# Moving the stores of the fp8 adjacency chunks back in SyncE's order in a four-layer graph network on Trainium2

## Chip, cores and metric

The kernel runs on one core of one Trainium2 chip. The metric is the device time of one launch in microseconds (us). Before the change the median of three runs is 6208.64 us (6201.9 to 6210.01).

## The reference, cut to what matters

There are 16 graphs of 1024 nodes with 128 features and a 0/1 adjacency matrix each. Four layers follow one another, each with a residual and a layer norm:

```
x = layernorm(x + softmax(masked relu-attention(x, adj)) @ v)                    # layer 0
x = layernorm(x + max over neighbours j of relu(p_i + q_j + b), adj as mask)     # layer 1
x = layernorm(x + MLP((1 + eps) * x + adj^T x))                                  # layer 2
adj_d = dilate(adj)      # row by row, earlier removals change the later rows
x = layernorm(x + (3 x (SAGE on adj_d, relu, batch norm), concatenated) @ Wl + bl)  # layer 3
```

`dilate` walks through the rows of a graph one after another: it counts a row's edges, and if there are more than ten it removes those whose rank is a multiple of half the count, symmetrically in the column. It depends on the adjacency alone, so it can run beside layers 0 to 2.

## The kernel before

**Slots.** Layers 0 to 2 and the dilation run together in one long stage. Its clock is layer 1. For every graph the 1024 neighbours are cut into 86 groups of 12 (`NP`, `PS`), and one group is one *slot*; 16 x 86 = 1376 slots are written out one after the other by `slot(s, last)` (L861). In a slot ScalarE (ACT) turns a matmul of the adjacency (`count`, L805, from the tile `AT`) into one-hot rows `hot`; TensorE (PE) looks up the maxima of neighbour subsets with them (`look_up`, L837, into the PSUM tile `pg`, two buffers); and VectorE (DVE) merges them into `best` (L908), twice per slot.

**Adjacency chunks.** `AT` holds 120 neighbours (ten slots' worth) by 1024 nodes in fp8. A graph has nine chunks (the ninth has 64 rows), so there are 144 in all, in four buffers. `load_columns(at)` (L753) is called every tenth slot with the number of the chunk that is needed about twenty slots later. It issues the load of that chunk from GpSimd (POOL), which also casts it from the f32 input to fp8, and on SyncE (SP) a store of the *previous* chunk to the DRAM copy `adj8` (L758), which the last layer reads long after (L995). A buffer of `AT` is free for chunk n+4 when the matmuls of chunk n are done and its store has landed.

**The dilation** (`dilation`, L500) goes through 32 row blocks of 32 rows (43 slots each). POOL decides the rows of a block one by one (L669 to L679), after DVE has made `low` and `rest` (L653, L655). Then SP stores `hit` (L686) and loads it back spread over the partitions as `hit_p` (L689), and DVE transposes it (`hit_T`, L703). While POOL works at block k, DVE finds the removed edges of block k-1 (`remove`, L573): the tile `gone` (L613, two buffers) goes to DRAM through SP (`removed`, L615), and its transpose `last_T` (L620) also (`removed_T`, L622). Later blocks load `gone_T` back (L517). `Vp` and `V` (L555, L556) also pass through SP.

**Other work of SP**: the loads of X, the rows of a graph (`load_x`, L745; three buffers, so a load follows the store of an older graph's X, L466). PE transposes X at L290.

**What sets the order.** PE, ACT, DVE and POOL run in this stage in the order in which the code is written (`tc.manual_schedule`); a planner inside the kernel (`ask`, `advance`) only decides where each small step is written. SP is not in that list: the framework's scheduler chooses the order of SP's instructions from their dependencies and an own estimate of time. SP then works through that order one after the other, and each DMA is issued when the semaphores that it waits for have come. The helper `behind(ins, start)` (L237) adds a dependency that counts in the scheduler's ordering alone, without a semaphore: the instructions emitted since `start` come behind `ins`.

Of the kernel before, what the change touches and what calls it, by code (L numbers as in the profile page):

```python
# [39 lines left out]
B, N, D, H2 = 16, 1024, 128, 256  # L40
P = 128
T = N // P
GS = 6
PS = 2 * GS
PC = 10
CH = PC * PS
# [28 lines left out]
def tile_graph_layers(ctx: ExitStack, tc, a, out):  # L75
    nc = tc.nc
# [95 lines left out]
    for b in range(B):  # L172
        q, g = divmod(b, G)
        nc.gpsimd.dma_start(out=half_rows[g * R:(g + 1) * R, :, q],
                            in_=a["nodemask"][b].rearrange("(k r) -> r k", r=R))
# [21 lines left out]
    adj8 = [dram.tile([N, N], F8, name=f"adj8_{b}") for b in range(B)]  # L197
# [39 lines left out]
    def behind(ins, start):  # L237
        for i in nc.cur_bb.bb.instructions[start:]:
            tc.add_manual_dep(i, ins.name, mybir.DependencyInfo(
                mybir.DependencyClass.NoSync, mybir.DependencyReason.SCHED_ONLY), reason="pace")  # L240

    def layers_012():
# [133 lines left out]
        def attend(b):  # L376
            for t in range(T):
                yield ask("PE", 0.01, after=("e", b, t))
                if t == 0:
                    y = w4.tile([P, T, D], F32, name="y0", tag="xT")  # L380
                e, total = exps.pop((b, t))
                eT = w4.tile([P, T, P], F32, name="eT")
                for h in range(2):
                    yield ask("PE", 0.44, take=True, same=(h == 0))
                    p = shared("pe")
                    for c in range(4):
                        nc.tensor.transpose(p[:, c * P:(c + 1) * P],  # L387
                                            e[:, (4 * h + c) * P:(4 * h + c + 1) * P], ident)
                    yield ask("A", 0.59, give=True, same=True)
                    nc.scalar.copy(eT[:, 4 * h:4 * h + 4, :].rearrange("p c i -> p (c i)"), p)  # L390
                happened["back", b, t] = now
                for h in range(4):
                    yield ask("PE", 0.45, take=(h == 0), same=(h > 0))
                    if h == 0:
                        pav = shared("pav")[:, :D]
                    for c in range(2 * h, 2 * h + 2):
                        nc.tensor.matmul(pav, eT[:, c, :], values[b][:, c, :], start=(c == 0), stop=(c == T - 1))  # L397
                yield ask("V", 0.4, give=True)
                share = small.tile([P, 1], F32, name="share")
                nc.vector.reciprocal(share, total)  # L400
                nc.vector.scalar_tensor_tensor(y[:, t, :], pav, share, X[b][:, t, :], op0=ALU.mult, op1=ALU.add)
            yield from norm(X[b], y)
            happened["X1", b] = now
# [66 lines left out]
        def tables_of(b):  # L470

            if b:
                yield ask("V", 0, urgent=True, after=("tables", b - 1))
            for g0 in range(0, NP, TG):
                n_g = 2 * min(TG, NP - g0)
                yield ask("V", 0.01, same=True, urgent=True, after=("q", b))
                made.append((b, g0))
                yield ask("V", 0.1, same=True, urgent=True, after=("used", *made[-3]) if len(made) > 2 else None)
                qg = qs[b].rearrange("o (g s) -> o g s", s=GS)
                subs[b, g0] = w2.tile([P, TG, P], F32, name="sub", bufs=2)  # L480
                sub = subs[b, g0].rearrange("o t (a s) -> o (t a) s", a=2)
                nc.vector.memset(sub[:, :n_g, 0:1], LOWEST)
                for k in range(GS):
                    n = 1 << k
                    yield ask("V", 0.06 + n * n_g / 960, same=(n < 8), urgent=True)
                    nc.vector.tensor_max(sub[:, :n_g, n:2 * n], sub[:, :n_g, 0:n],  # L486
                                         qg[:, 2 * g0:2 * g0 + n_g, k:k + 1].to_broadcast([P, n_g, n]))
                happened["sub", b, g0] = now
            happened["tables", b] = now
# [255 lines left out]
        def load_x(b):  # L745
            X[b] = apool.tile([P, T, D], F32, name="X", bufs=3)
            nc.sync.dma_start(out=X[b], in_=x[b].rearrange("(t p) d -> p t d", p=P))
# [4 lines left out]

        def load_columns(at):  # L753
            b, c = divmod(at, T + 1)
            if at:
                before, k = divmod(at - 1, T + 1)
                rows = min(CH, N - k * CH)
                nc.sync.dma_start(out=adj8[before][k * CH:k * CH + rows], in_=AT[at - 1][:rows])  # L758
            if b < B:
                rows = min(CH, N - c * CH)  # L760
                t = AT[at] = apool.tile([CH, N], F8, name="AT", bufs=4)
                if rows < CH:
                    nc.gpsimd.memset(t, 0.0)
                nc.gpsimd.dma_start(out=t[:rows], in_=adjT[b, c * CH:c * CH + rows])

        An, AT, subs, qs, ps, values, exps, bests, hots, tables = ({} for _ in range(10))
# [8 lines left out]
        def start(stream, first=False):  # L775
            pending[stream] = [next(stream, None), -9]
            streams.insert(0 if first else len(streams), stream)
# [59 lines left out]
        def look_up(s, h, pg):  # L837

            at = s % 2
            for k, part in enumerate(tables[s - at]):  # L840
                for a in range(2):
                    rows = slice(64 * a, 64 * a + 64)
                    nc.tensor.matmul(pg[:, a], part[rows, at * P:(at + 1) * P], hots[s][rows, halves[h]],  # L843
                                     start=(k == 0), stop=(k == 1))
# [5 lines left out]
        def total(b, h):  # L850
            s = halves[h]
            nc.vector.tensor_add(ps[b][:, s], bests[b][:, 0, s], ps[b][:, s])

        def dilate_on():
            nonlocal due, wants_bank
            if due <= now and not (wants_bank and taken >= 2 and given.get(taken - 2, 1e9) > now):
                after, cost, wants_bank = next(dilate, (B * NP, 0, False))
                due += after
                room["V"] -= cost

        def slot(s, last):  # L861

            nonlocal now
            now = s
            b, g = divmod(s, NP)
            if s >= 0 and g == 0:
                bests[b] = bests[b - 1] if b else w4.tile([P, 2, N], F32, name="best")
                if b + 1 < B:
                    start(tables_of(b + 1), True)
                    load_x(b + 1)  # L870
                    start(attend(b + 1))
                    start(scores(b + 1))
            if s >= 0 and g % PC == 0 and b * (T + 1) + g // PC + 2 <= B * (T + 1):
                load_columns(b * (T + 1) + g // PC + 2)
            for h in range(2):
                now = s + 0.5 * h
                for e in ROOM:
                    room[e] = min(room[e] + ROOM[e] / 2, ROOM[e] / (2 if e in ("PE", "V") else 1))
                if s >= 0:
                    pg = psum.tile([P, 2, 512], F32, tag="wide", name="pg", bufs=2)  # L880
                    look_up(s, h, pg)
                early = s >= 0 and due < now
                if early:
                    dilate_on()
                advance(("PE",))
                advance(("A", "V", "Pool"))
                if s >= 0 and not early:
                    dilate_on()
                if h == 0 and s % 2 and s + 1 < last:
                    low_part(s + 1)  # L890
                if s + 2 < last:
                    count(s + 2, h)
                    if h and s % 2 == 0:
                        table(s + 2)
                if s >= 0:
                    own = bests[b][:, :, halves[h]]
                    if g == 0:
                        if b:
                            if h:
                                merge(b - 1, h)  # L900
                            total(b - 1, h)
                        nc.vector.tensor_copy(own, pg)
                        if b and h:
                            start(rest(b - 1))
                    else:
                        if g == NP - 1 and h:
                            merge(b, 0)
                        nc.vector.tensor_max(own, own, pg)  # L908
            if s >= 0:
                hots.pop(s)  # L910
# [460 lines left out]
```

## Time and profile before

| | |
|---|---|
| median of three runs | 6208.64 us |
| profiled execution | 6199.75 us |
| its span | 6198.0 us, 93287 instructions |
| PE | busy 5582.7 us (90%) |
| DVE | busy 4870.0 us (79%) |
| ACT | busy 3988.2 us (64%) |
| POOL | busy 3613.1 us (58%) |
| merges L908 on DVE | 2720 x 1214 ns |
| AT loads L764 on POOL | 144, median 3.9 us from issue to landing |
| stores of AT on SP (L758) | 144, median 333 ns to issue |

The span is that of one execution as the hardware profiler took it. Busy times are per engine and overlap. SP's instructions are DMA issues and aren't counted as busy, but they have their own list of waits: how long SP stood before an issue, and which event released it. A line such as "DVE x L613 <- DMA y<-z: 80.6, 9, 18.0" says that DVE stood still before the instruction of L613 that writes x, 80.6 us in nine times, 18.0 at the longest, until a DMA that reads z and writes y had landed. The slot stage runs from about 140 to 5085 us; the last layer's passes follow.

### The profile page before, as it was taken

The numbers are of one execution on the slowest core, as the hardware profiler recorded it, in microseconds if no ns is written. First come the engines' busy times: TensorE is split into PE (matmuls) and PEld (weight loads), VectorE is DVE, ScalarE is ACT, GpSimd is POOL, SyncE is SP. The second block draws the span as 40 slices with busy tenths as digits, with TensorE's granted clock in tenths as the row PEclk, the third lists the DMA queues.
The fourth block names the chain that finished last, engine by engine and source line by source line (L and its number), as shares of the span: only waits on it lengthen the run. The fifth ranks groups of instructions, "written<-read, shape, count | busy, mean of one in ns | idle before, by whom it ended". The sixth has DMA issues, their size and how long they took to land.

```text
span 6198.0 us, 93287 instructions
## 1 busy us (share of the span) xinstructions
PE 5582.7 (90%) x30144; PEld 3046.0 (49%) x30250; DVE 4870.0 (79%) x7484; ACT 3988.2 (64%) x7362; POOL 3613.1 (58%) x11879
## 2 busy tenths in 40 slices
PE   5989899989898989999989798989999878999998
PEld 4545454545454545454545454545444435555654
DVE  3888788888888888889888788888889875555455
ACT  3767676767676767677767576767666554344855
POOL 2676666667666767677777757667677651110114
PEclk8999999989999999999999899999999989999999
DMA  5021213121212212122121211212121014554645
GB/s 42 11 33 25 40 22 42 22 40 24 40 24 31 32 32 32 32 32 38 26 43 22 39 24 31 31 31 33 31 33 28 19 41 124 159 144 133 214 163 191
DMA packets 496976, 334.28 MB, mean 54 GB/s; under 512 B 303338, under 2 KB 448228, under 8 KB 492388
## 3 DMA queue, kind: packets, MB, share of 16 engines
q1 hardware_dynamic: 405504, 260.29, 14.5%
q0 software_dynamic: 89008, 67.42, 12.6%
q8 instruction: 237, 3.88, 0.3%
q14 instruction: 255, 2.09, 0.1%
q10 hardware_dynamic: 1972, 0.59, 0.1%
HBM read 362.38 MB, written 133.96 MB: 80 GB/s over the span
## 4 chain that ended last, share of the span: by engine, by line
PE 31%; DVE 10%; ACT 4%; POOL 3%; issue 2%; DMA 1%; SPq 0%; DVEq 0%; POOLq 0%; ACTq 0%
PE pg L843 7%; PE pagg L1071 5%; DVE best L908 5%; PE pm L812 3%; PE po L1101 2%; PE po L1095 1%; PE pa L439 1%; PE pav L397 1%; PE pp L300 1%; ACT hot L813 1%; PE pdeg L1026 1%; DVE near L1014 1%; PE psc L349 1%; PE prank L599 1%; PE pe L387 1%
## 5 line engine op out<-in xcount | busy, mean ns | idle before, releaser
L908 DVE TENSOR_TENSOR best<-best,pg 128x1024 f32<-128x1024 f32 x2720 | 3259.3, 1214 | 512.6 <-PE pg L843 501.7
L813 ACT ACTIVATE hot<-pm,one_less 128x512 fp32r<-128x512 f32 x2752 | 1887.4, 689 | 780.5 <-PE pm L812 773.2
L843 PE MATMUL pg<-hot,high 64*128 64x512 f32 x5504 | 1407.3, 508 | 258.9 <-DVE best L908 220.8
L843 PE MATMUL pg<-hot,low 64*128 64x512 f32 x5504 | 1115.5, 402 | 0.0
L812 PE MATMUL pm<-AT,lit 120*128 120x512 fp8e4 x2752 | 1085.9, 395 | 4.5 <-ACT low L834 3.5
L843 PEld LDWEIGHTS pg<-hot,high 64*128 64x128 f32 x5504 | 523.5, 187 | 1014.6 <-DVE best L908 492.8
L669 POOL TENSOR_SCALAR sc<-low_counts,half_mask,rest 16x1 f32<-16x1 f32 x992 | 354.4, 357 | 393.9 <-DVE rest L655 283.2
L843 PEld LDWEIGHTS pg<-hot,low 64*128 64x128 f32 x5504 | 537.9, 192 | 0.0
L812 PEld LDWEIGHTS <-lit 120*128 120x128 fp8e4 x2752 | 270.3, 98 | 389.8 <-issue 313.5
L674 POOL TENSOR_SCALAR sc<-sc 16x1 f32<-16x1 f32 x992 | 393.1, 396 | 105.1
L834 ACT CAST low<-pt 128x256 fp32r<-128x256 f32 x688 | 256.0, 372 | 263.3 <-PE pt L832 261.9
L671 POOL TENSOR_SCALAR sc<-sc 16x1 f32<-16x1 f32 x992 | 324.5, 327 | 107.6
L1116 POOL TENSOR_TENSOR length<-length,mhalf 128x8 f32<-128x8 f32 x48 | 78.9, 1644 | 489.2 <-DVE length L1115 489.2
L676 POOL TENSOR_SCALAR hit<-V,sc 16x31 bf16<-16x31 bf16 (+30 forms) x992 | 362.4, 365 | 0.0
L677 POOL TENSOR_SCALAR last_rank<-V,sc 16x31 f32<-16x31 bf16 (+30 forms) x992 | 342.9, 346 | 0.0
L832 PE MATMUL pt<-high,less 128*128 128x256 f32 x688 | 279.2, 406 | 67.6 <-ACT high L827 61.5
L824 PE MATMUL pt<-ident,sub 128*128 128x128 f32 x1376 | 277.5, 283 | 51.8 <-ACT hot L813 50.0
L486 DVE TENSOR_TENSOR sub<-sub,q 128x24 f32<-128x24 f32 (+11 forms) x768 | 304.0, 397 | 24.8 <-ACT q L304 10.4
L397 PE MATMUL pav<-v,eT 128*128 128x128 f32 x2048 | 301.5, 292 | 2.0 <-ACT eT L390 2.0
L397 PEld LDWEIGHTS pav<-v,eT 128*128 128x128 f32 x2048 | 255.4, 196 | 73.3 <-issue 55.7
L670 POOL TENSOR_SCALAR sc<-sc 16x1 f32<-16x1 f32 x992 | 237.0, 239 | 86.5
L349 PE MATMUL psc<-kT,qT 128*128 128x256 f32 x1024 | 276.3, 388 | 9.9 <-issue 9.9
(270 smaller groups left out, 9662.9 us busy)
## 6 DMA issues: line engine op xcount, KB each, us to landing
removed<-gone SPq DMA_DIRECT2D x128, 256.0 KB
An<-in_adj_dram POOLq DMA_DIRECT2D x16, 1024.0 KB, 16.0
E<-in_adj_dram POOLq DMA_DIRECT2D x128, 128.0 KB, 6.6
gone_all<-removed POOLq DMA_DIRECT2D x64, 256.0 KB, 10.2
near<-adj SPq DMA_DIRECT2D x16, 1024.0 KB
kept<-near SPq DMA_DIRECT2D x16, 1024.0 KB
share<-share SPq DMA_DIRECT2D x32, 512.0 KB
hidden<-r SPq DMA_DIRECT2D x32, 512.0 KB
```

What stands on the lines that cost most here:

```text
L349: nc.tensor.matmul(psc[:, 256 * i:256 * (i + 1)], qT[:, t * P:(t + 1) * P], kT[:, s.start + 256 * i:s.start + 256 * (i + 1)], start=False, ...
L397: nc.tensor.matmul(pav, eT[:, c, :], values[b][:, c, :], start=(c == 0), stop=(c == T - 1))
L669: gp.tensor_scalar(half, mine, half_mask[:, m], rest[:, n:n + 1], op0=ALU.mult, op1=ALU.add)
L671: gp.tensor_scalar(sf, half, 5.5, sf, op0=ALU.is_gt, op1=ALU.mult)
L674: gp.tensor_scalar(to, at, sf, none, op0=ALU.subtract, op1=ALU.subtract)
L676: gp.tensor_scalar(hit[:, n, n + 1:], V[:, n, n + 1:], at, None, op0=ALU.is_equal)
L677: gp.tensor_scalar(last[:, n + 1:], V[:, n, n + 1:], to, None, op0=ALU.is_le)
L812: nc.tensor.matmul(pm, lit[:, r, :], AT[b * (T + 1) + c][:, halves[h]], start=True, stop=True)
L813: nc.scalar.activation(hots[s][:, halves[h]], pm, AF.Relu, bias=one_less)
L843: nc.tensor.matmul(pg[:, a], part[rows, at * P:(at + 1) * P], hots[s][rows, halves[h]], start=(k == 0), stop=(k == 1))
L908: nc.vector.tensor_max(own, own, pg)
L1071: nc.tensor.matmul(pa[:, s], piece[:, t, :], m[c][:, s], start=(i == 0), stop=(i == 15))
```

## The change

`load_columns(at)` now stores chunk at-2 in place of chunk at-1: a store is emitted in the call 20 slots after the one with its chunk's load, instead of 10. In addition the store is tied by `behind` to the last instruction emitted ahead of it, of whichever engine, so the scheduler can't place it earlier in SP's order than that instruction. As the stores lag one more call, the condition in `slot` that ended the calls at the last chunk is dropped, which leaves one further call at the end that only stores.

```
         def load_columns(at):
             b, c = divmod(at, T + 1)
-            if at:
-                before, k = divmod(at - 1, T + 1)
+            if at > 1:
+                before, k = divmod(at - 2, T + 1)
                 rows = min(CH, N - k * CH)
-                nc.sync.dma_start(out=adj8[before][k * CH:k * CH + rows], in_=AT[at - 1][:rows])
+                begin = len(nc.cur_bb.bb.instructions)
+                nc.sync.dma_start(out=adj8[before][k * CH:k * CH + rows], in_=AT[at - 2][:rows])
+                behind(nc.cur_bb.bb.instructions[begin - 1], begin)
             if b < B:
...
-            if s >= 0 and g % PC == 0 and b * (T + 1) + g // PC + 2 <= B * (T + 1):
+            if s >= 0 and g % PC == 0:
                 load_columns(b * (T + 1) + g // PC + 2)
```

From L758 on the line numbers of the changed kernel are larger by one or two: the store is L759, the load L766, the merge L910.

## The prediction

> **What bounds the kernel now.** The change touches only DMAs that SyncE (SP in the profile) issues, in the stage from about 140 to 5085 us in which the slots run. In that stage PE is busy 4487.33 of 4945 us, DVE 4252.78 and POOL 3390.61 (the busy times of that stretch). So PE and DVE take turns as the bound: 1376 slots in 4945 us are 3.59 us a slot, and each slot holds PE look-ups and two DVE merges (L908), which wait for each other through two PSUM buffers. In such a pair a pause of one engine stops the other within one or two half-slots. I therefore read the waits first, and only those whose releaser is a DMA, since SP orders DMAs and nothing else. The list of waits of DVE, then of PE and of POOL, in that stage (us in total, times, longest):
>
> ```profile
> DVE best L908 <- PE pg L843: 501.7, 848, 20.3
> DVE gone L613 <- DMA removed<-gone: 80.6, 9, 18.0
> DVE hit_T L703 <- DMA hit_p<-hit: 23.6, 2, 14.4
> ...
> PE ptr L290 <- DMA X<-in_x_dram: 28.7, 4, 20.3
> ...
> POOL counts L546 <- DVE U L544: 119.2, 13, 22.0
> ```
>
> DVE stands still 80.6 us in nine places because the tile `gone` that it wants to overwrite (two buffers) has not been stored; PE stands still 28.7 us because X has not come. Both transfers are issued by SP. SP's own waits, over the whole run:
>
> ```profile
> SPq L758 <- DMA AT<-in_adjT_dram: 2846.5, 138, 54.8
> SPq L686 <- POOL hit L678: 463.6, 24, 29.7
> SPq L615 <- DVE gone L613: 372.7, 47, 19.4
> ```
>
> SP spends 2846.5 us at the stores of AT (L758), each waiting for a load that has not even been issued. What is queued behind pays. The timelines of SP and then of DVE round one stall (start us, us, what; in brackets the idle time before it and its releaser):
>
> ```profile
> 1871.07 0.33 SPq L758 DMA_DIRECT2D adj<-AT  x1
> 1871.46 0.38 SPq L615 DMA_DIRECT2D removed<-gone  x1
> 1871.93 0.39 SPq L622 DMA_DIRECT2D removed_T<-last_T  x1
> 1908.75 0.45 SPq L758 DMA_DIRECT2D adj<-AT  x1
> 1909.30 0.54 SPq L615 DMA_DIRECT2D removed<-gone  x1
> ...
> 1895.84 1.21 DVE L908 TENSOR_TENSOR best<-best,pg 128x1024 f32<-128x1024 f32 x1
> 1911.94 0.55 DVE L613 TENSOR_SCALAR gone<-rank,least,match 128x1024 bf16<-128x1024 f16 x1 [14.89 <-DMA removed<-gone]
> ```
>
> SP issues nothing from 1872.3 to 1908.75. The `gone` finished at 1868.4 is stored only at 1909.30, and DVE waits 14.89 us for it; PE's look-ups have a gap of 14.9 us there too. Likewise for X:
>
> ```profile
> 3524.22 0.34 SPq L466 DMA_DIRECT2D x<-X  x1
> 3548.01 0.32 SPq L758 DMA_DIRECT2D adj<-AT  x1
> 3548.43 0.40 SPq L747 DMA_DIRECT2D X<-in_x_dram  x1
> ...
> 3561.55 1.11 PE L290 MATMUL ptr<-ident,X 128*128 128x128 f32 x4 [20.32 <-DMA X<-in_x_dram]
> ```
>
> [...] during those 36 us no later SP transfer is issued although its data is ready. [...] here a look-up pair that takes 0.50 us takes 0.80 us directly after the 16.4 us gap at 650 us.
>
> **The change part by part.**
> (1) *Stores move back in SP's order.* In the program as built PE, DVE, ACT and POOL hold the same instructions in the same order as before. SP's 1082 other transfers keep their order too; only the 144 stores move, by 0 to 22 other transfers, 9 at the median. No instruction is added or removed, so the issue cost of 144 x about 0.33 us stays on SP.
> To price the move I went through SP's new order with the readiness times of the trace of before: the end of `gone` (L613), of `last_T` (L620), Vp (L552), the last `hit` of a row block (L678), and the POOL issue of each AT load plus its 3.9 us to landing (the median of the profile); an issue takes 0.45 us. The same walk over the old order meets the measured issues within 1.5 us for 95% of most kinds. Over the new order:
> - SP waits for an AT load at two of the 144 stores only (the first, and one at 391 us that nothing ready stands behind), against 138 before.
> - The `removed` stores are issued on average 9.0 us earlier, by up to 41 us. Before, 67 of 128 were over 3 us late; one stays so, in the last row block, where it stands behind `hit`. The nine DVE waits need at most 18.0 us. Each goes: **-80.6 us**.
> - The X loads of 3548.4 and 3869.6 us go out 21.5 and 20.0 us earlier. PE's two long waits for X in this stage are 20.3 us (at 3561.6) and 8.0 us (at 3874.4). X then lands at 3526.9 + 13.1 = 3540.0 by the landing time of before (3548.4 to 3561.5), and PE wants it at 3541.2: both go: **-28.3 us**.
> (2) *Does a removed stall shorten the run by as much?* Row blocks of the dilation take 43 slots each, and the nine `gone` stalls lie in nine of the 32 blocks. From `rest` (L655) to the next `rest`, those nine (blocks 3, 5, 7, 9, 11, 13, 19, 25, 27) take 165.7, 154.7, 160.3, 155.6, 159.7, 161.1, 147.3, 157.0 and 157.0 us; less their own stalls (18.0, 4.8, 9.1, 7.4, 14.9, 11.8, 4.7, 4.2, 5.8) they average 148.6. The five odd blocks without one from 15 on (15, 17, 21, 23, 29) average 149.0. So nothing is caught up after a stall, and I take one for one. [...]
> (3) *The wait that stays.* `hit_T`'s 23.6 us (9.3 at 408.8, 14.4 at 5045.6) comes from POOL, which ends its rows at 402.8 and 5040.0; SP issues `hit` at once both times. **0**.
> (4) *The longer hold of AT's buffers.* There are four. The load of chunk n+4, issued by POOL, needs the store of chunk n. In the walk that store is issued at least 9.9 us (chunk 7), in all other cases at least 27.6 us before POOL comes to the load (before: 100.6). A store of 120 KB that lands in the 3.9 us of its load is out of the way. **0**; if this cover is gone, POOL stands still in its row loop.
> (5) *SP traffic between `hit` and `hit_p`*, which DVE soon needs: a few AT stores now stand there, 0.45 us each, against slacks at `hit_T` of over 2 us in the blocks concerned: **0 to +5 us**. From below, [...] the few small waits for late stores: **-10 to 0**. They roughly cancel; I take 0.
>
> Sum: -80.6 - 28.3 = **-108.9 us**. The profiled execution of before took 6199.75 us (span 6198.0), so its like after is 6090.8. The median of the three runs is 6208.64, 8.9 above that execution; from it the change gives 6208.64 - 108.9 = 6099.7, so **6100 us**.
>
> **The rivals.**
> *A. POOL takes back much of it.* After a row block's 31 POOL rows come `hit`, `hit_p` and DVE's `hit_T`. In the stall blocks `hit_T` starts only 3.5 to 10.6 us after the last `hit_p` is issued, and a landing takes about 2.8. If POOL kept its times, DVE would wait there for what the stall exceeds that slack by: 16.1, 2.0, 2.2, 5.5, 14.2, 10.8, 0.3, 0.7 and 0 us, together 51.8. The gain is then 57 us: 6152 us. For it: POOL's row loop takes about 118 us of a block and is near the bound. Against it: POOL itself waits for DVE in just these blocks (the L546 line above; 22.0 us in block 3, 16.7 in block 11). Less its waits, POOL needs 115.1 to 119.9 us there, plus about 5.7 for both transfers (2.9 to the last issue, 2.8 to land), while `hit_T` would come 125 to 137 us after `rest`. Hence small.
> *B. Slower: POOL is held at AT loads.* A store now stands nearer the load that reuses its buffer, and where it is queued behind `hit` (SP waits there for POOL up to 29.7 us) a load may find its buffer taken. POOL issues in order, so its rows, `hit_T` and then DVE are late. It decides from the point where stores run 10 us (one chunk) or 28 us (the rest) later than the walk says. At 5 us in each of 32 blocks it costs 160 us: 6099.7 + 160 = 6260 us. Against it: those margins, and that all SP work in the walk gets earlier.
> *C. The stalls have another cause* [...], and one wait replaces another: no change, about 6207 us. Against it: in the nine stalls SP's preceding issue is an AT store, within 3 us of the stall's end.
>
> **How the numbers follow.** The main case gets 0.80 (its own range 6080 to 6125), A 0.14 (6125 to 6160), C 0.02, B 0.04. A measurement of this kernel tells about 0.2%, 12 us, from no change. Faster: 0.80 + 0.14 = 0.94; same 0.02; slower 0.04. The range runs from 6072 (the -10 of part 5, and as much again for small waits that go too) to 6150, just short of A's worked point.
>
> **What would show it.** Right: in the profile after, "DVE gone <- DMA removed" and the 20 us wait of PE for X are gone, SP's waits at AT stores fall from 2846 us to under 150, and the slot stage ends near 4976 instead of 5085. A shows as more than 40 us of "DVE hit_T <- DMA hit_p"; B as POOL waiting for "DMA adj<-AT" at L766. It is wrong if these stalls go and the stage is not about 100 us shorter.

## The result and the profile after

The changed kernel takes 6095.76 us (median of 4 runs, 6090.76 to 6098.93) against 6207.42 us before (4 runs): a ratio of 0.9821, 95% interval 0.9804 to 0.9838, or 111.7 us less. The profiled execution took 6090.76 us, its span 6089.0 us, 109.0 us less than before. Of these, 107.2 us lie in the slot stage: its last merge (L908, now L910) ends at 4982.0 us in place of 5089.3.

The waits of DVE from 140 to 5085 us, the window of before, which now takes in some 100 us of the last layer (in total, times, longest):

```profile
DVE best L910 <- PE pg L845: 470.4, 839, 8.8
DVE hit_T L703 <- DMA hit_p<-hit: 26.2, 2, 15.7
```

The line "DVE gone L613 <- DMA removed<-gone", 80.6 us before, has vanished. PE's list for the stage has no wait for X any more (28.7 us before). On DVE that wait of PE had shown as a wait for look-ups: its first line is 31.3 us shorter (501.7 to 470.4). So DVE's own list closes the account: 80.6 + 31.3 less the 2.6 us by which `hit_T` grew are 109.3 us. POOL's list:

```profile
POOL num L707 <- DVE counts L530: 289.6, 31, 21.6
POOL sc L669 <- DVE rest L655: 285.0, 30, 15.5
...
POOL counts L546 <- DVE U L544: 27.4, 11, 6.8
```

Its wait at L546, 119.2 us before, has shrunk to 27.4, so most of it was an echo of the stalls. SP's own list over the whole run:

```profile
SPq L615 <- DVE gone L613: 1874.2, 119, 53.9
SPq L686 <- POOL hit L678: 724.4, 24, 76.0
...
SPq L759 <- DMA AT<-in_adjT_dram: 41.5, 2, 34.1
```

SP waits nearly as long as before (5522 us against 5664, all lines of its list added up), but for something else: it stands at the store of `gone` until DVE has made it. That delays nobody: `hit_T` is the only wait for an SP transfer that DVE and PE still have in the stage. The 2846.5 us at the stores of AT have become 41.5 us, in the two places that the walk named. The timeline of SP in the row block of the prediction's example:

```profile
1813.79 0.34 SPq L615 DMA_DIRECT2D removed<-gone  x1
1815.67 0.38 SPq L622 DMA_DIRECT2D removed_T<-last_T  x1
1816.15 1.14 SPq L759 DMA_DIRECT2D adj<-AT  x1
1823.89 0.33 SPq L615 DMA_DIRECT2D removed<-gone  x1
```

Each `removed` goes out at once (DVE starts these two `gone` at 1813.2 and 1823.3 us, each takes 0.54 us), and SP issues the store of AT behind them without a wait for its load. Of the 128 `removed` stores 67 were over 3 us late before; now one is, in the last row block, as the walk said. The X load that was 21.5 us late now follows the store of the older X within 3 us and stands ahead of the AT store:

```profile
3451.25 0.34 SPq L466 DMA_DIRECT2D x<-X  x1
3453.98 0.40 SPq L747 DMA_DIRECT2D X<-in_x_dram  x1
3454.47 0.54 SPq L759 DMA_DIRECT2D adj<-AT  x1
```

### The profile page after: what moved, and what is told of

The parts are those of the page before. It is cut to its first block, busy times and chain, and to the rows that moved or that the text cites. A ratio compares the mean times of both kernels' runs of the same rounds, so it can differ in the third digit from the quotient of the medians.

```text
span 6089.0 us, 93282 instructions
## 1 busy us (share of the span) xinstructions
PE 5556.8 (91%) x30144; PEld 3035.5 (50%) x30250; DVE 4873.7 (80%) x7484; ACT 3992.1 (66%) x7362; POOL 3642.6 (60%) x11879
## 4 chain that ended last, share of the span: by engine, by line
PE 33%; DVE 11%; ACT 4%; issue 2%; POOL 1%; DMA 1%; SPq 0%; DVEq 0%; ACTq 0%; POOLq 0%
PE pg L845 8%; DVE best L910 5%; PE pagg L1073 5%; PE pm L814 3%; PE po L1103 2%; PE pa L439 1%; PE po L1097 1%; PE pav L397 1%; PE pp L300 1%; ACT hot L815 1%; DVE sub L486 1%; PE prank L599 1%; PE pdeg L1028 1%; DVE near L1016 1%; PE pe L387 1%
## 5 line engine op out<-in xcount | busy, mean ns | idle before, releaser
L910 DVE TENSOR_TENSOR best<-best,pg 128x1024 f32<-128x1024 f32 x2720 | 3260.8, 1215 | 481.2 <-PE pg L845 470.4
```

## The experiments

The theory: SP works through its order one after the other (36 us without an issue in the prediction's example), and an AT store ahead of its load holds up the `removed` stores and X loads behind it; DVE and PE then stand still, one for one. The rivals: POOL's chain takes the gain back (A), POOL is held at AT loads (B), another wait takes the place (C).

### The lag alone

Against the changed kernel one line goes; the lag of two calls stays:

```
                 nc.sync.dma_start(out=adj8[before][k * CH:k * CH + rows], in_=AT[at - 2][:rows])
-                behind(nc.cur_bb.bb.instructions[begin - 1], begin)
```

> The store is emitted a call later (chunk at-2), but not tied. Built so, SP holds its transfers in the same order as before the change: the scheduler puts the stores back ahead. If what counts is SP's order (my theory), nothing changes: about 6207 us, SP waits some 2850 us at the stores, DVE some 80 us for removed<-gone. If the later emission itself counts (buffers, POOL's loads), the time goes to about 6097 us.

Measured: 6201.39 us beside 6201.5 us of before on that chip, ratio 0.9997 (0.9988 to 1.0007). Its waits, DVE's in the stage and SP's in the run:

```profile
DVE gone L613 <- DMA removed<-gone: 84.8, 10, 18.1
...
SPq L759 <- DMA AT<-in_adjT_dram: 2859.5, 138, 55.2
```

Writing the store ten slots later in the code does nothing: SP is outside the manual schedule, and the scheduler puts the store back where it stood. In the trace SP's 1226 transfers come in exactly the order of before.

### The tie alone

Against the kernel before:

```
+                begin = len(nc.cur_bb.bb.instructions)
                 nc.sync.dma_start(out=adj8[before][k * CH:k * CH + rows], in_=AT[at - 1][:rows])
+                behind(nc.cur_bb.bb.instructions[begin - 1], begin)
```

> The store keeps its lag of one call (chunk at-1), but is tied behind the place where it is emitted. Going through SP's order as built with the readiness times of the changed kernel, SP waits about 110 us in all at the stores (24 of 144) and no ready transfer stands behind for long. My theory: all of the gain, 6090 to 6100 us. If the lag of 20 slots is needed, some of the stalls of DVE for gone return: 6120 us or more.

Measured: 6106.6 us, ratio 0.9838 (0.9817 to 0.9858), beside 6201.5 us of before on that chip: 94.9 us less; the interval is 88 to 113 us. No wait of DVE for `gone` or of PE for X is left, and at the stores SP waits:

```profile
SPq L759 <- DMA AT<-in_adjT_dram: 87.5, 24, 11.3
```

So the tie carries the change. The changed kernel's ratio, 0.9821, is 0.17% lower, but the two intervals overlap widely; whether the second lag adds a little stays open. This run also answers a doubt. In the profiled execution of the changed kernel PE is busy 23.7 us less in the slot stage than before (4465.1 us against 4488.8), and the mean granted clock of that stage is 0.98 in place of 0.96, so the clock could have had a part in the gain. With the tie alone PE is busy 4490.3 us there, no less than before (granted clock 0.965 over the whole execution, against 0.962 in the trace of before), and the stage still ends 92.6 us earlier (at 4996.7 us).

### The tie in the first half of the graphs

As the tie alone, but only the chunks of graphs 0 to 7 are tied:

```
+                if before < 8:
+                    behind(nc.cur_bb.bb.instructions[begin - 1], begin)
```

> The tie (lag of one call) only for the chunks of graphs 0 to 7; the others as before. In the walk through SP's order the stalls of DVE for gone up to 2220 us go (18.0 + 4.8 + 9.1 + 7.4 + 14.9 + 11.8 = 66.0 us), and those at 3111, 4052 and 4360 us and PE's two waits for X stay. If each stall counts one for one: 6207 - 66 = 6141 us. If a stall removed is caught up elsewhere (POOL's row loop), the gain is well under 50 us: 6160 us or more.

Measured: 6143.59 us, ratio 0.9907 (0.989 to 0.9923), 57.9 us less; the interval is 48 to 68 us. What stays of the waits in the stage, DVE's and then PE's:

```profile
DVE gone L613 <- DMA removed<-gone: 19.8, 5, 6.1
...
PE ptr L290 <- DMA X<-in_x_dram: 27.5, 2, 19.7
```

The six stalls up to 2220 us are gone and the three later ones are there, as expected. Two new ones of 2.7 and 2.0 us came up in the second half (at 4456 and 4620 us), so 60.8 us of DVE's waits for `gone` went, not 66.0.

### The tie in graphs 10 to 12

As the tie alone, but only for these graphs:

```
+                if 10 <= before <= 12:
+                    behind(nc.cur_bb.bb.instructions[begin - 1], begin)
```

> The tie (lag of one call) only for the chunks of graphs 10 to 12. In the walk PE's two waits for X (20.3 + 8.0 us) and the stall of DVE for gone at 4052 us (4.2 us) go, all others stay: 6207 - 32.5 = 6174.5 us if the X waits are SP's queue and count one for one. If X comes late for another reason (its buffer is freed late, or the DMA engines are busy), PE still waits for X and the time is about 6203 us.

Measured: 6164.38 us, ratio 0.994 (0.9924 to 0.9956), 37.1 us less; the interval is 27 to 47 us. PE's waits for X in the stage go. DVE's for `gone` hardly change in sum:

```profile
DVE gone L613 <- DMA removed<-gone: 80.0, 9, 18.2
```

The stall at 4052 us did go, but a new one of 2.8 us came at 4636 us. So X came late because its load stood behind a store in SP's queue. The two parts together take 57.9 + 37.1 = 95.0 us away, the tie on all graphs 94.9 us on the same chip. That these agree to 0.1 us is luck: the two parts leave the stalls near 3111 and 4360 us (4.7 and 5.8 us) in place, and each figure is uncertain by about 10 us. Within that the gain adds up stall by stall, and nothing shows that much of it is caught up elsewhere.

### The changed kernel on the chip of the next three runs

> The changed kernel itself, on the same chip as the other runs of this set: some 0.982 of before (6096 us where before takes 6207 us).

Measured: 6093.08 us, ratio 0.9815 (0.98 to 0.983), with 6210.66 us for before. DVE's wait for `hit_p` in this execution:

```profile
DVE hit_T L703 <- DMA hit_p<-hit: 28.9, 4, 17.0
```

### The stores on ACT's queue

Against the kernel before:

```
-                nc.sync.dma_start(out=adj8[before][k * CH:k * CH + rows], in_=AT[at - 1][:rows])
+                nc.scalar.dma_start(out=adj8[before][k * CH:k * CH + rows].bitcast(F32), in_=AT[at - 1][:rows].bitcast(F32))
```

> The stores (lag of one call, no tie) are issued by ACT, whose order is the written one, in place of SP; the bytes are viewed as f32. SP's other transfers keep their order and have no store among them. If what matters is that a store stands ahead of ready transfers in SP's queue (my theory), the stalls for gone and X go as in the changed kernel: 6090 to 6120 us, the upper end if ACT's 144 issues at SP's 0.33 us each (48 us) are not hidden. If the time at which the store is made or its data moves were the cause, nothing of the kind follows.

Measured: 6140.6 us, ratio 0.9896 (0.9882 to 0.9911): 47.5 us more than the changed kernel beside it. DVE's waits for `gone` and PE's for X are gone, as the theory says. What came instead are two long waits of ACT, in its timeline (the second with SP's beside it):

```profile
4477.38 0.32 ACTq L758 DMA_DIRECT2D adj<-AT  x1
4477.75 1.15 ACT L337 ACTIVATE off<-An,ones 128x1024 bf16<-128x1024 fp8e4 x1 [25.27 <-DMA hit_p<-hit]
...
4955.07 0.33 SPq L686 DMA_DIRECT2D hit<-hit  x1
...
4956.72 0.37 ACTq L758 DMA_DIRECT2D adj<-AT  x1
4957.14 1.27 ACT L813 ACTIVATE hot<-pm,one_less 128x512 fp32r<-128x512 f32 x2 [38.81 <-DMA hit<-hit]
```

The profile puts the end of both waits down to the landing of an SP transfer. At 4956.72 that is SP's `hit` of 4955.07; at 4477.38 it is a load of `hit_p`, which SP issued from 4475.71 on, behind the `hit` of 4474.15. Both `hit` had waited for POOL: SP's list books its waits ahead of all 32 of them to POOL (24 times L678, 733.4 us, and 8 times L679, 339.7 us). The stores of AT read nothing that these transfers write, and the chunk to be stored at 4956.72 had landed at 4903.8. So ACT waited for POOL through transfers of SP's queue; what ties its stores to their landings is not shown. The two waits are 64.1 us. DVE's wait for `hit_p` is 18.8 us shorter in return (28.9 us in the changed kernel on this chip, 10.1 us here), and 64.1 - 18.8 = 45.3 us is about the difference of 47.5. That leaves next to nothing for the 144 issues themselves. So one wait did take the place of another, as in rival C, not in the lists of the changed kernel but in the variant that looks simplest.

### The store as late as it can be

Against the changed kernel, as is the next one:

```
-            if at > 1:
-                before, k = divmod(at - 2, T + 1)
+            if at > 3:
+                before, k = divmod(at - 4, T + 1)
...
-                nc.sync.dma_start(out=adj8[before][k * CH:k * CH + rows], in_=AT[at - 2][:rows])
+                nc.sync.dma_start(out=adj8[before][k * CH:k * CH + rows], in_=AT[at - 4][:rows])
...
+            load_columns(B * (T + 1) + 2)
+            load_columns(B * (T + 1) + 3)
```

> As the changed kernel, but chunk at-4 is stored, directly ahead of the load into its buffer. In the walk through SP's order 37 of 140 loads find their buffer not yet stored, for 145 us in all. Rival B of the prediction, made to happen: POOL waits about 145 us for adj<-AT. If POOL's slack ahead of hit_T (0.2 to 15 us a row block) takes it up, 6100 us; I expect that about a third comes through as waits of DVE for hit_p or as late POOL results, 6120 to 6150 us.

Measured: 6096.06 us, ratio 0.9818 (0.98 to 0.9836), within the spread of the changed kernel (6093.08 us on this chip): the expected 20 to 50 us did not come. POOL did wait. Its list for the stage:

```profile
POOL sc L669 <- DVE rest L655: 272.2, 29, 15.5
POOL num L707 <- DVE counts L530: 212.0, 28, 22.5
POOL AT L766 <- PE pg L845: 50.9, 28, 6.2
POOL AT L766 <- PE pm L814: 40.2, 23, 12.0
...
POOL AT L766 <- DMA adj<-AT: 21.3, 6, 9.0
...
POOL AT L765 <- DMA adj<-AT: 16.6, 4, 8.0
...
POOL counts L546 <- DVE U L544: 5.3, 3, 2.6
```

The four AT lines sum to 129.0 us, against 17.5 us of the two PE ones in the first trace of the changed kernel, which has none for adj<-AT. (Two are booked to PE; a wait for several events is booked to the one that came last by the profile, and PE is where it was in the changed kernel, so these too are waits for the store, by inference.) But 77.6 us came out of POOL's wait at L707 (289.6 to 212.0) and 22.1 out of the one at L546 (27.4 to 5.3). DVE's wait for `hit_p` stayed at 26.1 us. So POOL would have waited for DVE later anyway, and most of the new waits only took the place of those.

### The stall that the change leaves

```
+            moved = {0: -4, 1: 4, 28: -1.5, 29: -2, 30: -2, 31: 5.5}
...
-                yield (B * NP - 10) / K - 36.93, 0.65, False
+                yield (B * NP - 10) / K - 36.93 + moved.get(k, 0), 0.65, False
```

> The changed kernel with the place of hit_T moved in six of the 32 row blocks, in slots: block 0 by -4, block 1 by +4, blocks 28, 29, 30 by -1.5, -2, -2, block 31 by +5.5 (the sum is 0). The two waits of DVE for hit_p that the change leaves (10.5 us in block 1, 15.7 us in block 31) come from POOL's rows being too slow for these two blocks; earlier blocks have slack to give. If they count one for one, 20 to 26 us less than the changed kernel: 0.978 of before. If POOL takes it back in the blocks that are shortened, no change against the changed kernel.

Measured: 6071.58 us, ratio 0.9782 (0.9769 to 0.9796), 21.5 us less than the changed kernel on the same chip; the two intervals do not overlap (that of the changed kernel begins at 0.98). DVE's wait for `hit_p`:

```profile
DVE hit_T L704 <- DMA hit_p<-hit: 0.5, 1, 0.5
```

This version is faster than both kernels. The blocks that gave slots had slack in POOL's chain, as the changed kernel's trace shows (15 us between the landing of `hit_p` and `hit_T` in block 0, 6 to 10 us in blocks 28 to 30).

## Why the prediction was right, point by point

- **Part 1, the stores' place in SP's order.** Right in kind and size: the walk said waits at two stores (41.5 us measured), no stall of DVE for `gone` (80.6 to 0) and none of PE for X (28.7 to 0). The lag-alone run shows that SP's order is what counts: the store is written later, SP's order stays, and so do the stalls and the time.
- **Part 2, one for one.** Forecast 108.9 us; the span fell by 109.0 us, the median by 111.7 us (101 to 122 by the ratio's interval). One for one is shown to about 10 us; that the span meets the forecast to 0.1 us is luck, since executions of one kernel differ by 8 us. The partial ties, 57.9 us where 66.0 us were forecast and 37.1 us where 32.5 us were, agree with one for one within their intervals.
- **Part 3, `hit_T` stays.** 23.6 became 26.2 us. The re-timed run confirms its cause, POOL's rows in two blocks.
- **Part 4, AT's buffers.** No wait of POOL for adj<-AT in the changed kernel. The prediction said that POOL would stand still if this cover were gone. In the late-store run it did, for over 100 us more than in the changed kernel, and this cost nothing that could be measured.
- **Part 5** was put at 0 to +5 and, as an estimate of the author's without a sum behind it, at -10 to 0 us; the 2.6 us at `hit_T` lie in the first, and nothing separates the second from the spread of runs: PE's busy time in the stage fell by 23.7 us in the changed kernel's first trace and rose by 1.5 us with the tie alone.
- **Rival A** did not come: its sign was more than 40 us of waits for `hit_p`, and there were 26.2 us, in the same two blocks as before. POOL's wait at L546 shrank by 91.8 us, so POOL kept pace. Its fear had a ground, since two blocks are bound by POOL, but not the nine with stalls.
- **Rival B** was priced wrongly. It charged 5 us in each of 32 blocks in full to the end. In the late-store run POOL's AT waits were 129.0 us, 4 us a block, and its wait in front of L707 gave up 77.6 us of it.
- **Rival C** was wrong about this change: the stalls went, and `hit_T`'s wait grew by 2.6 us alone. Another wait did take their place where ACT issued the 144 stores: ACT stood still 64.1 us for landings of SP's transfers, and the run took 47.5 us more than the changed kernel.

## What to carry to other kernels

SP, which only issues DMAs here, shows no busy time in these profiles. Its waits were harmful or harmless by what stood behind them (2846.5 us at the AT stores before, 1874.2 us at the stores of `gone` after): read for each long wait of the queue what was ready behind it, and price the change by who waited for that. Where the scheduler orders such a queue, moving the line in the code may change nothing (6201.39 us against 6201.5 with the lag alone); look at the order that was built. When DMAs move to another engine's queue, read in its list of waits which landings that engine then waits for: here two of SP's transfers, 64.1 us.

## What was not expected of the hardware and its software

POOL at 60% busy (3642.6 us of 6089.0) looked co-critical by row block, yet took about 110 us more of waits without a measurable loss. And a DMA on ACT's queue stood still for 38.8 us with its data ready, until a transfer of SP's queue had landed.
